# A merged attention-and-edge stage on one core: product buffers, a bank for projections, and the distance between steps

## The chip, the cores and the metric

The kernel runs on one core of one Trainium2 chip. A core has a matrix engine (PE, with its weight loads shown apart as PEld), a vector engine (DVE), a scalar engine (ACT), a general engine (POOL), and a sync engine (SP) that issues most of the direct DMAs here. The matrix engine writes its results to PSUM, which has eight banks of 2 KB in each of its 128 partitions. DVE and ACT read the results from there. The metric is the time of one execution on the device, in microseconds, as the median of several runs.

## The reference, cut to what matters

Two layers of a graph network work on 32768 nodes of 256 numbers and 524288 edges. The edges come sorted by `dst`.

```python
# layer 0: 256 graphs of 128 nodes, 8 heads of 32
h = relu(layernorm(x))
Q, K, V = h @ Wq + bq, h @ Wk + bk, h @ Wv + bv
attn = softmax(Q K^T / sqrt(32) + edge_bias)       # per graph and head; all edges fall to graph 0
x = x + (attn V) @ Wo + bo
# layer 1
h = relu(layernorm(x)); h = batchnorm(h)           # statistics over all nodes
a_in  = segment_sum((h @ W_in  + b_in )[src] * w_in,  dst)
a_out = segment_sum((h @ W_out + b_out)[dst] * w_out, src)
xi = concat(a_in, a_out) @ W_x2i + b_x2i;  hh = h @ W_h2h
gate = sigmoid(xi_i + hh_i); new = tanh(xi_n + hh_n)
x = x + new + gate * (h - new)
```

## The kernel before, in words

The kernel has four stretches. First it builds edge tables and the bias of graph 0. Then comes the merged stage, which the change is about. Then it adds up the messages per node, and at last it computes the gates.

The merged stage does two things at once. Attention works on groups of 512 nodes (`GB` = 4 graphs). The outgoing edges are handled at the same time: an *item* is 128 edges whose `dst` lie in one block of 128 nodes, 64 items (`CI`) make a round, and 4352 items are worked on in all. A loop of `turns` (L1133 onward) takes four rounds a trip (`UG`), or one. Each round carries the attention of one group (`attend`, L834) and the projections of the next group (`project`, L743), as long as groups are left; the last rounds have items alone. The edges come in three parts, and `spread` runs once for each.

Inside a trip the order of the work on PE, DVE, ACT and SP is written out by hand (`manual_schedule`); POOL is left out of that. The body is a Python loop over steps `t`, and one step starts one item. What an item needs is done at fixed lags, given by the tuple `steps` (L1130): at lag 0 SP fetches 128 rows of the normalised features (`fetch`, tile `hb`); at 4 PE spreads lane numbers to all partitions, for four items at once (`spread_lanes`, tile `bc`); at 6 DVE compares (`select`, tiles `selT` and `oh`); at 8 PE counts (`rank`), PE picks the rows of each edge (`product`, tile `mp`), and DVE reads the place of each edge (`place`, tile `jk`); at 9 ACT scales the product by the edge weight (`scale`, tile `msg`) and POOL scatters finished messages to memory (`scatter`). In one step, each engine runs what the tuple gives, from left to right, and then the attention work that `at(t)` put down for that step. An engine takes its instructions strictly in this order.

The places come from running counts `R`, which live in PSUM. There are two copies, in two tiles of their own, and item `i` uses copy `i % 2`. The rank of item `i` adds three matmuls to its copy:

```python
add("ones_b", i - 1, i, turn)     # R[i % 2] += all of item i - 1
add("triu", i - 2, i, turn)       # R[i % 2] += the rest of item i - 2
add("tri", i, i, turn)            # R[i % 2] += what stands before each edge of item i
```

Then `place` reads `R[i % 2]` on DVE. So the next matmul that touches the copy which item `i` reads is the first one of item `i + 2`.

PSUM is full: `mm`, `sc` and `pt` for attention and projections (one bank each), `bc`, two buffers of `mp`, and the two copies of `R`. The projections of the coming group borrow the banks of attention: transposed inputs and half of the queries and keys in `mm`, the other half in `pt`, values in `pt` and `sc`. In attention, a step's result is mostly read in the next step: scores (L849), their maximum (L857), the exponentials (L863), their transposes (L869), and so on.

Of the kernel before, what the change touches and what calls it, by code (L numbers as in the profile page):

```python
# [499 lines left out]
def gnn_kernel(ctx, tc, x, src, dst, edge_attr, edge_type, w_in_e, w_out_e,  # L500
# [186 lines left out]
    with ExitStack() as c1:  # L687
# [56 lines left out]
        def project(g, qT, kbd):  # L744
# [7 lines left out]
            for b in range(GB):  # L752
                cols = slice(b * P, (b + 1) * P)
                row = {}

                @at(9 + b // 2)
                def _(b=b):
                    row_stats(0, b, xg[:, b])

                @at(17 + 2 * b)  # L760
                def _(b=b, row=row):
                    xn = row["xn"] = ab.tile([P, D], F32, name="xn")
                    nc.vector.tensor_scalar(xn, xg[:, b], mv[0][:, b, 0:1], rstd[0][:, b:b + 1],
                                            op0=ALU.subtract, op1=ALU.mult)

                @at(18 + 2 * b)
                def _(row=row):
                    row["tp"] = transposed("mm", row["xn"])

                @at(19 + 2 * b)  # L770
                def _(row=row, cols=cols):
                    nc.scalar.activation(hT[:, :, cols], row["tp"], AF.Relu)
# [9 lines left out]
            for m in range(KC):  # L782
                ps = {}
                mc = slice(m * P, (m + 1) * P)
                bank = ("pt", "mm")[m]
                for k in range(KC):
                    @at(26 + 7 * m + k)
                    def _(m=m, k=k, ps=ps, mc=mc, bank=bank):
                        if k == 0:
                            ps["q"] = a_ps.tile([P, GN], F32, name=bank)  # L790
                        nc.tensor.matmul(ps["q"], wq[:, k, mc], hT[:, k], start=(k == 0), stop=(k == KC - 1))

                    @at(29 + 7 * m + k)
                    def _(m=m, k=k, ps=ps, mc=mc, bank=bank):
                        if k == 0:
                            ps["k"] = a_ps.tile([P, GN], F32, name=bank)
                        nc.tensor.matmul(ps["k"], wk[:, k, mc], hT[:, k], start=(k == 0), stop=(k == KC - 1))

                @at(28 + 7 * m)
                def _(m=m, ps=ps):  # L800
                    nc.scalar.activation(qT[:, m], ps["q"], AF.Identity, bias=bq_c[:, m:m + 1], scale=SCALE)

                for j in range(HC):
                    @at(31 + 7 * m + j // 2)
                    def _(m=m, j=j, ps=ps):
                        r = slice(j * DH, (j + 1) * DH)
                        to = kbd[r, m, :, j, :]
                        of = ps["k"][r].rearrange("p (b n) -> p b n", b=GB)
                        if j % 2:
                            nc.scalar.activation(to, of, AF.Identity, bias=bk_c[r, m:m + 1])  # L810
                        else:
                            nc.vector.tensor_scalar(to, of, bk_c[r, m:m + 1], None, op0=ALU.add)


            for b, t, bank in ((0, 41, "pt"), (2, 59, "sc")):
                ps = {}
                for i in range(2):
                    @at(t + i)
                    def _(b=b, i=i, ps=ps, bank=bank):
                        if i == 0:  # L820
                            ps["v"] = a_ps.tile([P, 2, D], F32, name=bank)
                        for k in range(KC):
                            nc.tensor.matmul(ps["v"][:, i], hT[:, k, (b + i) * P:(b + i + 1) * P], wv[:, k],
                                             start=(k == 0), stop=(k == KC - 1))

                @at(t + 2)
                def _(b=b, ps=ps):
                    nc.scalar.copy(vg[:, b:b + 2, :, 0:DH], ps["v"].rearrange("p b (h d) -> p b h d", d=DH))

            @at(63)  # L830
            def _():
                nc.gpsimd.tensor_add(xb, xg, bo_b[:, None, :].to_broadcast([P, GB, D]))
# [3 lines left out]
        def attend(g, qT, kbd, bias=None):  # L836

            todo, at = steps_of()
            for b in range(GB):
# [3 lines left out]
                for m in range(KC):  # L843
                    hs = slice(m * HC, (m + 1) * HC)

                    @at(B + 4 * m)
                    def _(b=b, m=m, s=s, cols=cols, hs=hs):
# [5 lines left out]

                    @at(B + 1 + 4 * m)
                    def _(m=m, s=s):
                        s["nm", m] = ab.tile([P, HC], F32, name="nm")
                        nc.vector.tensor_reduce(s["nm", m], s["sc", m], AX.X, ALU.max, negate=True)  # L857
                        s["pr", m] = ab.tile([P, HC, P], F32, name="pr")

                    for j in range(HC):  # L860
                        @at(B + (2, 6)[m] + j // 2)
                        def _(m=m, j=j, s=s):
                            nc.scalar.activation(s["pr", m][:, j], s["sc", m][:, j], AF.Exp, bias=s["nm", m][:, j:j + 1])  # L863

                        @at(B + (3, 7)[m] + j // 2)
                        def _(m=m, j=j, s=s):
# [3 lines left out]

                    @at(B + (6, 9)[m])
                    def _(m=m, s=s):
# [5 lines left out]

                    @at(B + 10 + m)
                    def _(b=b, m=m, s=s):  # L880
# [5 lines left out]

                @at(B + 12)
                def _(s=s):
# [19 lines left out]

                @at(B + 16)
                def _(b=b, s=s):  # L910
# [7 lines left out]

                @at(B + 17)
                def _(bs=bs):  # L920
                    std(1, bs)

                @at(B + 18)
                def _(bs=bs):
# [4 lines left out]
                for n, u in enumerate(range(bs.start, bs.stop)):  # L929
                    h = {}  # L930

                    @at(B + 18 + 2 * n)
                    def _(u=u):
                        nc.scalar.activation(h1g[:, u], x1g[:, u], AF.Relu, bias=nmr[:, u:u + 1], scale=rstd[1][:, u:u + 1])
# [9 lines left out]
            @at(B + 17)  # L944
            def _():
                nc.scalar.dma_start(x1_g[g], x1g)

            @at(B + 19)
            def _():
                nc.sync.dma_start(h1_g[g], h1g)  # L950

            @at(B + 21)
            def _():
# [35 lines left out]
        zm = fp.tile([P, T3 // P, MW], F32, name="zmsg")  # L989
        nc.vector.memset(zm, 0.0)  # L990
        nc.vector.memset(zm[:, :, FW:FW + 1], -1.0e6)
# [15 lines left out]
        def spread(k, lo, hi):  # L1007
# [7 lines left out]
            w0_1, node_1 = itp[k]  # L1015
            nc.scalar.dma_start(msg_d[k][hi - lo:hi - lo + T3].rearrange("(p e) w -> p e w", p=P), zm)
            for r in R:
                nc.tensor.matmul(r, cn["row0"], soff[k], start=True, stop=False, skip_group_check=True)

# [68 lines left out]
            def product(i, q, c, turn):  # L1088
                mp = turn["mp", i] = pp.tile([P, D], F32, name="mp")
                nc.tensor.matmul(mp, turn["sel", i // 4][:, q % 4], turn.pop(("hb", i)), start=True, stop=True)  # L1090

            def add(what, of, to, turn):
                oh = turn["oh", of]
                nc.tensor.matmul(R[to % 2], cn[what], oh, start=False, stop=False, skip_group_check=True)  # L1094

# [14 lines left out]
            def place(i, q, c, turn):  # L1110
                if q % 4 == 0:
                    c["pf"] = ip.tile([P, 4], F32, name="pf")
                jk = sp.tile([P, NB], F32, name="jk")
                nc.vector.scalar_tensor_tensor(jk, cn["iota1"], c["ed"][:, 0, q:q + 1], R[i % 2], op0=ALU.is_equal,  # L1114
                                               op1=ALU.mult, accum_out=c["pf"][:, q % 4:q % 4 + 1])
# [330 lines left out]
```

## Time and profile before

| what | us |
|---|---|
| median of 3 runs | 17105.49 (17104.96 to 17109.16) |
| the profiled execution | 19598.35 |
| its span, first to last instruction | 19596.6 |
| merged stage in the span, from and to | 1059 to 10047 |
| of it, rounds with attention (63) | 1059 to 9417 |
| of it, rounds of items alone (5) | 9417 to 10047 |
| a trip of four rounds with attention | 511 to 530 |
| a trip of one round, with attention / without | 128 to 149 / 122 to 126 |

The profiled execution takes 14.6% longer than the median run, so its times are not those of an ordinary run one by one. A row of the profile names the line of the kernel, the engine, what is written and read, how often, the busy time and the mean of one in nanoseconds, and then the time that the engine sat idle just before, with what ended most of that idle time. "issue" means that no wait visible to the profile ended there. PE's busy time counts the filling of its pipeline: matmuls that start 0.11 us apart are each shown with 0.27 us.

### The profile page before, as it was taken

To read this page: it belongs to the slowest core of one execution; us is meant where nothing else is said; L and a number is where in the kernel's file an instruction comes from. 1 tells how busy PE (TensorE), PEld (TensorE's weight loads), DVE (VectorE), ACT (ScalarE), POOL (GpSimd) and SP (SyncE) were. 2 spreads that over 40 slices of the span, in tenths; PEclk is the share of its full clock that TensorE was granted. 3 is DMA by queue.
4 is the path that set the end of the run, shared out by engine and by line. 5 is a ranking of instruction groups with operands and counts; after the bars stand their busy time and mean duration, and the time that the engine had idled before them with its cause. 6 is when DMAs were issued, how large, how long until landed. Compare 5 with 4: busy or idle time off the path is not lost. (4 is left out here: it accounts for less than half of the span.)

```text
span 19596.6 us, 292930 instructions
## 1 busy us (share of the span) xinstructions
PE 14917.0 (76%) x71786; PEld 10574.5 (54%) x71786; DVE 10035.6 (51%) x33823; ACT 6877.9 (35%) x17011; POOL 9326.3 (48%) x9309
## 2 busy tenths in 40 slices
PE   2078777777887777887668778777877777788889
PEld 2055555555555555555446666666666666653334
DVE  8656666566666656665444444444444444432222
ACT  0044444444444444444223333333333333320000
POOL 0045555445455445554555555555555555542222
PEclk6589989889888888988779999899999999999999
DMA  2044444444444434444446777677776777773332
GB/s 65 6 136 149 147 149 149 137 140 147 142 149 146 139 124 144 143 147 139 132 142 194 193 197 196 184 197 198 196 194 187 196 196 197 197 155 113 105 112 96
DMA packets 1829641, 2975.64 MB, mean 152 GB/s; under 512 B 299498, under 2 KB 1288135, under 8 KB 1827670
## 3 DMA queue, kind: packets, MB, share of 16 engines
q1 hardware_dynamic: 1203190, 1584.46, 27.5%
q0 software_dynamic: 430768, 1160.40, 20.5%
q10 hardware_dynamic: 194096, 212.95, 3.5%
q8 instruction: 590, 9.67, 0.2%
q14 instruction: 997, 8.17, 0.1%
HBM read 2124.16 MB, written 1248.64 MB: 172 GB/s over the span
## 5 line engine op out<-in xcount | busy, mean ns | idle before, releaser
L1123 POOL DMA_INDIRECT msg_d<-msg,pi x4352 | 4308.2, 990 | 3816.3 <-ACT msg L1106 1527.1
L1252 POOL DMA_INDIRECT rows<-h_d,ixc x3584 | 3407.5, 951 | 2331.8 <-issue 743.4
L1114 DVE SCALAR_TENSOR_TENSOR jk<-iota,edc,R 128x256 f32<-128x256 bf16 x4352 | 2072.8, 476 | 3059.3 <-remote 928.6
L1287 ACT ACTIVATE selo<-lane_row,sl 128x128 f32<-128x128 f32 x5040 | 1661.6, 391 | 4691.3 <-DVE sl L1284 1574.9
L1294 PE MATMUL ps_o<-m,selo 128*128 128x257 f32 x10080 | 2757.9, 413 | 645.7 <-ACT selo L1288 293.7
L1106 ACT ACTIVATE msg<-mp,edc 128x256 f32<-128x256 f32 x4352 | 2048.1, 477 | 3415.4 <-PE mp L1090 1522.5
L1266 PE MATMUL ps_i<-rows,sel 128*128 128x257 f32 x8960 | 2617.6, 412 | 761.6 <-DVE acc L1270 381.2
L1090 PE MATMUL mp<-hb,selT 128*128 128x256 f32 x8704 | 2926.6, 421 | 342.1 <-ACT msg L1106 145.7
L1294 PEld LDWEIGHTS ps_o<-m,selo 128*128 128x128 f32 x10080 | 1969.6, 205 | 1050.9 <-issue 312.5
L1266 PEld LDWEIGHTS ps_i<-rows,sel 128*128 128x128 f32 x8960 | 1627.5, 205 | 1054.7 <-DVE acc L1270 429.3
L1259 DVE TENSOR_SCALAR sel<-lane_row,ed 128x128 f32<-128x128 f32 x4480 | 1395.9, 360 | 973.2 <-PE idle L1267 374.7
L1090 PEld LDWEIGHTS mp<-hb,selT 128*128 128x128 f32 x8704 | 1460.2, 210 | 570.5 <-ACT msg L1106 230.9
L1094 PE MATMUL R<-oh,ones_b 128*128 128x256 bf16 x4352 | 1275.4, 293 | 635.6 <-issue 318.5
L1298 DVE SCALAR_TENSOR_TENSOR acc<-acc,blk,ps_o 128x257 f32<-128x257 f32 x1680 | 805.5, 479 | 1412.9 <-PE ps_o L1294 571.2
L1086 DVE TENSOR_SCALAR oh<-iota,edc 128x256 bf16<-128x256 bf16 x4352 | 1360.0, 313 | 2.0
L1094 PE MATMUL R<-oh,triu 128*128 128x256 bf16 x4352 | 1273.4, 293 | 10.5 <-DVE jk L1114 10.5
L1094 PE MATMUL R<-oh,tri 128*128 128x256 bf16 x4352 | 1272.2, 292 | 0.0
L1270 DVE SCALAR_TENSOR_TENSOR acc<-acc,blk,ps_i 128x257 f32<-128x257 f32 x2240 | 1070.0, 478 | 300.3 <-DMA sin_d<-acc 76.8
L1252 POOL DMA_INDIRECT rows<-h_d,ixh x896 | 852.2, 951 | 635.7 <-issue 247.2
L1284 DVE TENSOR_SCALAR sl<-m,blk 128x3 f32<-128x3 f32 x1680 | 416.6, 248 | 1372.4 <-DMA m<-msg_d 1139.5
L1094 PEld LDWEIGHTS <-triu 128*128 128x128 bf16 x4352 | 447.7, 103 | 1163.8 <-issue 1017.5
L1288 ACT ACTIVATE selo<-selo,one 128x384 f32<-128x384 f32 x1680 | 1031.1, 614 | 52.2
(372 smaller groups left out, 21051.9 us busy)
## 6 DMA issues: line engine op xcount, KB each, us to landing
m<-msg_d SPq DMA_DIRECT2D x1680, 396.0 KB
hb<-h_d SPq DMA_DIRECT2D x4352, 128.0 KB
sin_d<-acc SPq DMA_DIRECT2D x2240, 128.5 KB
sout_d<-acc SPq DMA_DIRECT2D x1680, 128.5 KB
msg_d<-msg,pi POOLq DMA_INDIRECT x4352
more<-sout_d ACTq DMA_DIRECT2D x128, 514.0 KB
rows<-h_d,ixc POOLq DMA_INDIRECT x3584
xg<-in_x SPq DMA_DIRECT2D x65, 512.0 KB
```

Of the source, the lines that this page charges most:

```text
L1086: nc.vector.tensor_scalar(oh, cn["iota1"], c["ed"][:, 0, q:q + 1], None, op0=ALU.is_equal)
L1090: nc.tensor.matmul(mp, turn["sel", i // 4][:, q % 4], turn.pop(("hb", i)), start=True, stop=True)
L1094: nc.tensor.matmul(R[to % 2], cn[what], oh, start=False, stop=False, skip_group_check=True)
L1106: nc.scalar.activation(msg[:, q % 4, 0:D], turn.pop(("mp", i)), AF.Copy, scale=c["ed"][:, 1, q:q + 1])
L1114: nc.vector.scalar_tensor_tensor(jk, cn["iota1"], c["ed"][:, 0, q:q + 1], R[i % 2], op0=ALU.is_equal, op1=ALU.mult, accum_out=c["pf"][:, q ...
L1123: s = nc.gpsimd.indirect_dma_start(out=msg_d[k][:], out_offset=bass.IndirectOffsetOnAxis(ap=c["pi"][:, j:j + 1], axis=0), in_=msgs[i // 4 ...
L1252: nc.gpsimd.indirect_dma_start(out=rows[(2 * i + r) % NR][:, 0:D], out_offset=None, in_=h1_d[:], in_offset=bass.IndirectOffsetOnAxis(ap=(i ...
L1259: nc.vector.tensor_scalar(sel[:, r], cn["lane_row"], c["ed"][:, 0, r, i:i + 1], c["ed"][:, 1, r, i:i + 1], op0=ALU.is_equal, op1=ALU.mult)
L1266: nc.tensor.matmul(ps, sel[:, r], rows[(2 * i + r) % NR], start=(r == 0), stop=(r == 1))
L1270: nc.vector.scalar_tensor_tensor(acc[0][i % NA], acc[0][(i - 1) % NA], c["blk"][:, 0, i:i + 1], c.pop(("t_ps", i)), op0=ALU.mult, op1=ALU.add)
L1287: nc.scalar.activation(sel[:, r], cn["lane_row"], AF.Abs, bias=sl[:, r:r + 1])
L1294: nc.tensor.matmul(ps, sel[:, r], m[:, r, 0:FW], start=(r == 0), stop=(r == T3 // P - 1))
```

## The change

The change touches the merged stage only.

- The product tile `mp` holds two products of 256 numbers, so that two tiles (two banks) hold four products. An even item takes a new tile, an odd one the second half of the same tile.
- The two copies of `R` become the halves of one tile, in one bank, written at the start by one matmul of 512 columns.
- The bank that this sets free is the tile `mx`. The projections (transposes, queries, keys, values) and the transposes of the normalised output rows use it and leave `mm`, `pt` and `sc` to attention.
- Rows are fetched 12 steps ahead of the product (`LEAD`), with 14 buffers in place of 10. The other lags keep their distance to the product.
- In `attend` and `project` two or three steps lie between an instruction that makes a value and the one on another engine that reads it, mostly in place of one.
- The one-hot tile `oh` has 7 buffers in place of 8, and the block of zeros `zm`, written once per part, is stored once and repeated by the DMA's pattern.

```diff
 # project
-                @at(17 + 2 * b)          # xn on DVE
+                @at(13 + 3 * b)
-                @at(18 + 2 * b)
+                @at(15 + 3 * b)
                 def _(row=row):
-                    row["tp"] = transposed("mm", row["xn"])
+                    row["tp"] = transposed("mx", row["xn"])
-                @at(19 + 2 * b)
+                @at(16 + 3 * b)
                 def _(row=row, cols=cols):
                     nc.scalar.activation(hT[:, :, cols], row["tp"], AF.Relu)
...
-                bank = ("pt", "mm")[m]
-                    @at(26 + 7 * m + k)
+                    @at(27 + 10 * m + k)
-                            ps["q"] = a_ps.tile([P, GN], F32, name=bank)
+                            ps["q"] = a_ps.tile([P, GN], F32, name="mx")
-                    @at(29 + 7 * m + k)
+                    @at(31 + 10 * m + k)
-                            ps["k"] = a_ps.tile([P, GN], F32, name=bank)
+                            ps["k"] = a_ps.tile([P, GN], F32, name="mx")
-                @at(28 + 7 * m)
+                @at(29 + 10 * m)
-                    @at(31 + 7 * m + j // 2)
+                    @at(33 + 10 * m + j // 2)
...
-            for b, t, bank in ((0, 41, "pt"), (2, 59, "sc")):
+            for b, t in ((0, 47), (2, 67)):
-            @at(63)
+            @at(67)
 # attend
-                    @at(B + 4 * m)                       # scores
+                    @at(B + 5 * m)
-                    @at(B + 1 + 4 * m)                   # maximum
+                    @at(B + 1 + 5 * m)
-                        @at(B + (2, 6)[m] + j // 2)      # exponentials
+                        @at(B + 2 + 5 * m + j // 2)
-                        @at(B + (3, 7)[m] + j // 2)      # transposes
+                        @at(B + 4 + 5 * m + j // 2)
-                    @at(B + (6, 9)[m])                   # copies PT
+                    @at(B + (6, 11)[m])
-                    @at(B + 10 + m)                      # attention times values
+                    @at(B + 12 + m)
-                @at(B + 12)                              # division
+                @at(B + 14)
-                @at(B + 13)                              # transposes
+                @at(B + 16)
-                @at(B + 14)                              # copy oT
+                @at(B + 17)
-                @at(B + 15)                              # times Wo
+                @at(B + 19)
-                @at(B + 16)                              # residual, statistics
+                @at(B + 20)
-                    @at(B + 18 + 2 * n)                  # normalised rows
+                    @at(B + 23 + 3 * n)
-                    @at(B + 19 + 2 * n)
+                    @at(B + 25 + 3 * n)
                     def _(u=u, h=h):
-                        h["tp"] = transposed("mm", h1g[:, u])
+                        h["tp"] = transposed("mx", h1g[:, u])
-                    @at(B + 20 + 2 * n)
+                    @at(B + 26 + 3 * n)
...
 # items
+        LEAD = 12
-        op = c1.enter_context(tc.tile_pool(name="p_o", bufs=8))
+        op = c1.enter_context(tc.tile_pool(name="p_o", bufs=7))
-        hp = c1.enter_context(tc.tile_pool(name="p_h", bufs=10))
+        hp = c1.enter_context(tc.tile_pool(name="p_h", bufs=14))
-        R = [p1.tile([P, NB], F32, name=f"R{i}") for i in range(2)]
+        R = p1.tile([P, 2, NB], F32, name="R")
...
-                mp = turn["mp", i] = pp.tile([P, D], F32, name="mp")
+                if i % 2 == 0:
+                    turn["mp"] = pp.tile([P, 2, D], F32, name="mp")
+                mp = turn["mp", i] = turn["mp"][:, i % 2]
...
-                nc.tensor.matmul(R[to % 2], cn[what], oh, start=False, stop=False, skip_group_check=True)
+                nc.tensor.matmul(R[:, to % 2], cn[what], oh, start=False, stop=False, skip_group_check=True)
...
-            steps = ((0, fetch), (4, spread_lanes), (6, select), (8, rank), (8, product), (8, place), (9, scale), (9, scatter))
+            steps = ((0, fetch), (LEAD - 4, spread_lanes), (LEAD - 2, select), (LEAD, rank), (LEAD, product), (LEAD, place),
+                     (LEAD + 1, scale), (LEAD + 1, scatter))
```

More of the change, by code (lines that the diff above doesn't have):

```diff
@@ L784, in project, with _ @@
                 mc = slice(m * P, (m + 1) * P)
-                bank = ("pt", "mm")[m]
                 for k in range(KC):
-                    @at(26 + 7 * m + k)
-                    def _(m=m, k=k, ps=ps, mc=mc, bank=bank):
+                    @at(27 + 10 * m + k)
+                    def _(m=m, k=k, ps=ps, mc=mc):
                         if k == 0:
-                            ps["q"] = a_ps.tile([P, GN], F32, name=bank)
+                            ps["q"] = a_ps.tile([P, GN], F32, name="mx")
                         nc.tensor.matmul(ps["q"], wq[:, k, mc], hT[:, k], start=(k == 0), stop=(k == KC - 1))
-                    @at(29 + 7 * m + k)
-                    def _(m=m, k=k, ps=ps, mc=mc, bank=bank):
+                    @at(31 + 10 * m + k)
+                    def _(m=m, k=k, ps=ps, mc=mc):
                         if k == 0:
-                            ps["k"] = a_ps.tile([P, GN], F32, name=bank)
+                            ps["k"] = a_ps.tile([P, GN], F32, name="mx")
                         nc.tensor.matmul(ps["k"], wk[:, k, mc], hT[:, k], start=(k == 0), stop=(k == KC - 1))
-                @at(28 + 7 * m)
+                @at(29 + 10 * m)
                 def _(m=m, ps=ps):
@@ L818, in _ @@
                     @at(t + i)
-                    def _(b=b, i=i, ps=ps, bank=bank):
+                    def _(b=b, i=i, ps=ps):
                         if i == 0:
-                            ps["v"] = a_ps.tile([P, 2, D], F32, name=bank)
+                            ps["v"] = a_ps.tile([P, 2, D], F32, name="mx")
                         for k in range(KC):
@@ L917, in attend @@
                 bs = slice(0, b + 1) if b < GB - 1 else slice(b, b + 1)
-                @at(B + 17)
+                @at(B + 21)
                 def _(bs=bs):
                     std(1, bs)
-                @at(B + 18)
+                @at(B + 22)
                 def _(bs=bs):
@@ L930, in attend @@
                     h = {}
-                    @at(B + 18 + 2 * n)
+                    @at(B + 23 + 3 * n)
                     def _(u=u):
                         nc.scalar.activation(h1g[:, u], x1g[:, u], AF.Relu, bias=nmr[:, u:u + 1], scale=rstd[1][:, u:u + 1])
-                    @at(B + 19 + 2 * n)
+                    @at(B + 25 + 3 * n)
                     def _(u=u, h=h):
-                        h["tp"] = transposed("mm", h1g[:, u])
-                    @at(B + 20 + 2 * n)
+                        h["tp"] = transposed("mx", h1g[:, u])
+                    @at(B + 26 + 3 * n)
                     def _(u=u, h=h):
                         nc.scalar.copy(h1T[:, :, u * P:(u + 1) * P], h["tp"])
-            @at(B + 17)
+            @at(B + 21)
             def _():
                 nc.scalar.dma_start(x1_g[g], x1g)
-            @at(B + 19)
+            @at(B + 24)
             def _():
                 nc.sync.dma_start(h1_g[g], h1g)
-            @at(B + 21)
+            @at(B + 28)
             def _():
@@ L988, in gnn_kernel @@
         p1 = c1.enter_context(tc.tile_pool(name="p_p1", bufs=1, space=PSUM))
-        zm = fp.tile([P, T3 // P, MW], F32, name="zmsg")
+        zm = fp.tile([P, MW], F32, name="zmsg")
         nc.vector.memset(zm, 0.0)
-        nc.vector.memset(zm[:, :, FW:FW + 1], -1.0e6)
+        nc.vector.memset(zm[:, FW:FW + 1], -1.0e6)
         eno = fp.tile([CI, T1], F32, name="eno")
         nc.gpsimd.iota(eno, pattern=[[1, T1]], base=0, channel_multiplier=0, allow_small_or_imprecise_dtypes=True)
-        R = [p1.tile([P, NB], F32, name=f"R{i}") for i in range(2)]
+        R = p1.tile([P, 2, NB], F32, name="R")
         win = fp.tile([CI, T1 * 4], F32, name="win")
@@ L1015, in spread @@
             w0_1, node_1 = itp[k]
-            nc.scalar.dma_start(msg_d[k][hi - lo:hi - lo + T3].rearrange("(p e) w -> p e w", p=P), zm)
-            for r in R:
-                nc.tensor.matmul(r, cn["row0"], soff[k], start=True, stop=False, skip_group_check=True)
+            nc.scalar.dma_start(msg_d[k][hi - lo:hi - lo + T3].rearrange("(p e) w -> p e w", p=P),
+                                zm[:, None, :].to_broadcast([P, T3 // P, MW]))
+            nc.tensor.matmul(R, cn["row0"], soff[k][:, None, :].to_broadcast([soff[k].shape[0], 2, NB]), start=True,
+                             stop=False, skip_group_check=True)
             def derive(c):
@@ L1113, in place @@
                 jk = sp.tile([P, NB], F32, name="jk")
-                nc.vector.scalar_tensor_tensor(jk, cn["iota1"], c["ed"][:, 0, q:q + 1], R[i % 2], op0=ALU.is_equal,
+                nc.vector.scalar_tensor_tensor(jk, cn["iota1"], c["ed"][:, 0, q:q + 1], R[:, i % 2], op0=ALU.is_equal,
                                                op1=ALU.mult, accum_out=c["pf"][:, q % 4:q % 4 + 1])
```

## The prediction, made before the changed kernel ran

> **What bounds the kernel now.** First I read the page's groups to see what a step costs, then the busy time by stretch, to place the merged stage.
>
> ```profile
> core 0: us, PE busy (x) PEld busy (x) DVE busy (x) ACT busy (x) POOL busy (x), PEclk, DMA share, GB/s
> 1058.00:3653.00 2595.00, 2075.19 (x11437) 1397.16 (x11437) 1621.60 (x5978) 1210.33 (x3021) 1325.69 (x1316) 0.91 0.47 149
> 10047.00:17400.00 7353.00, 5774.64 (x26865) 4863.27 (x26866) 3233.94 (x10368) 2648.05 (x6686) 4262.74 (x4485) 0.92 0.71 193
> ```
>
> The first row is five trips of four rounds: 2595 us for 20 rounds, so 129.7 us a round of 64 steps and 2.03 us a step. No engine is full: PE 80%, DVE 62%, POOL 51%, ACT 47%. The bound is in the waits. So next come the waits of PE between 1059 and 9418, where it stands idle 1754 us in all.
>
> ```profile
> PE R L1094 <- DVE jk L1114: 282.6, 205, 7.1
> PE R L1094 <- issue: 222.9, 118, 5.2
> PE sc L849 <- PEq L1135: 191.2, 15, 17.1
> PE pt L869 <- issue: 157.5, 91, 3.2
> PE mp L1090 <- ACT msg L1106: 137.5, 163, 2.3
> PE mm L741 <- DVE xn L763: 133.3, 40, 5.8
> PE mp L1090 <- issue: 96.3, 135, 2.4
> PE pt L869 <- ACT pr L863: 63.7, 90, 2.6
> PE mp L1090 <- ACT kbd L810: 63.0, 57, 1.8
> PE mm L741 <- ACT h1g L934: 62.7, 63, 3.5
> ...
> PE pt L869 <- ACT msg L1106: 37.4, 40, 2.0
> PE mm L741 <- DVE nm L857: 34.7, 28, 4.5
> ```
>
> Two kinds matter. PE waits for a result of the step before (xn, pr, h1g, nm; msg and kbd where ACT was late to free a product bank): the rows shown with a producer give 532 us, with o (18.3) and PT (10.8) 561 us. And its counting matmuls wait for DVE to have read R: 283 us, with only part of the 223 us of "issue". The rows of back-edges (191 us) the change leaves alone. Row fetches: in the whole stage PE idles 2.4 us for them, seven times.
>
> The last view is time order in rounds of items alone: the hand-over of R, both ways.
>
> ```profile
> 9707.09 0.27 PE L1094 MATMUL R<-oh,tri 128*128 128x256 bf16 x1
> 9707.40 0.48 DVE L1114 SCALAR_TENSOR_TENSOR jk<-iota,edc,R 128x256 f32<-128x256 bf16 x1
> ...
> 9712.14 0.48 DVE L1114 SCALAR_TENSOR_TENSOR jk<-iota,edc,R 128x256 f32<-128x256 bf16 x1 [3.75 <-remote]
> ...
> 9712.68 0.27 PE L1094 MATMUL R<-oh,ones_b 128*128 128x256 bf16 x1 [2.92 <-issue]
> ```
>
> From tri to DVE's read: 0.31 us. From the start of the read to the waiting matmul: 0.54. Three counting matmuls start 0.11 apart. A closed loop PE, DVE, PE thus takes 0.22 + 0.31 + 0.54 = 1.07 us. Today it may span two steps, because item i + 1 counts in another bank.
>
> **A rule of the skill, weighed.** The Trainium skill, "PSUM — Partial Sum Buffer", section "PSUM bank collisions raise a hardware error", says that two different engines must not be at one bank and one group of 32 partitions at once, even on disjoint columns, so software has to order them. The halves of the new R are disjoint columns of one bank on the same partitions. The trace of before shows the ordering done even more broadly: four reads of a key projection take different partitions of one bank, and ACT's reads follow DVE's, 0.03 to 0.09 us after they end. This is who waits for the DVE reads of L812:
>
> ```profile
> who waited for it (us, times):
>   ACT kbd L810: 430.7, 199
> ```
>
> I go by the rule: item i + 1 may not count before item i's place has been read. The three-matmul ping-pong stays, but the slack that it bought shrinks from two steps to one. The same holds for a product pair: ACT's scale of an even item must follow PE's product of the odd one.
>
> **The change, part by part**, against the profiled 19598 us (span 19597 and 2 around it), and then carried to the median.
>
> *R in one bank.* I lay the after schedule over 64 steps, with start-to-start pitches from the trace at full clock. PE: counting 3 x 0.109, product 2 x 0.216, spreading 0.22 every fourth step, scores 0.86, half of a block's attention 0.89, Wo 0.86, query or key part 0.86, a values part 0.86, a transpose 0.11. DVE: read 0.40, one-hot 0.19, selT 0.66 every fourth, maximum 0.59, PT 0.60, key copies 0.66 each, residual with statistics about 1.0, derive about 0.16 a step. PE sums to 86 us a round, DVE to 74. If neither can run ahead, a step costs the larger of PE, DVE and 1.07: the sum is 104.6. With today's schedule and pairs of steps, it is 97.2. The difference is 7.5 us a round, 0.12 us a step. A second reading agrees: among the 1555 steps whose read came within 0.6 us of tri, the next item's first matmul now starts before the point that the rule allows in 48%, by 0.12 us on the mean over all of them. Bounds: nothing, if product and attention (at least 0.43 us on PE) always cover the read; 104.6 - 86 = 18.6 us a round, 0.29 a step, if today's slack hides everything. I take 0.12 x 4352 = +507 us. Behind a waiting counting matmul stand the product, then the attention of that step; for the product waits ACT's scale, then POOL's scatter, which is idle half its time.
>
> *Steps farther apart, `mx`, four products.* These remove the 561 us at best (with the "issue" rows of pt, mp and mm, 315 us more, if they are the same thing); at worst nothing, as PE then meets the next wait. After the change PE has more work than DVE in 43 of 64 steps; in the others what it gains at a transpose it waits at the next counting. I take 0.6: -337 us. ACT waiting for the odd product costs nothing by itself: the attention results it makes later are read two steps on.
>
> *Twelve steps of lead.* The fetch is hidden already, so no gain. A trip has 4 more steps at its head with no counting; those carry attention, not waiting. At 26 trips and 0.4 us a light step: +42 us; from nothing to 100. SP issues the same 4352 fetches, four earlier, and the buffer of a fetch is freed two steps before in both versions (10 - 8, 14 - 12). POOL's scatters and window gathers are issued in the same order.
>
> *The rest.* Seven one-hot buffers leave three steps between last use and refill, covered by DVE's two steps of distance; the zeros are written three times in all; the wide first matmul of R happens three times. Nothing.
>
> Sum: 507 - 337 + 42 = +212 us on the profiled time. The median run is 14.6% shorter; the same share gives 212 / 1.146 = +185: 17,290 us. The forecast turns where R costs (337 - 42) / 4352 = 0.07 us a step.
>
> **Rivals.** A change within 0.2% (34 us) can't be told from none.
>
> 1. *Faster: the read is covered.* Attention on PE fills 0.6 us of a mean step beside the product's 0.43, and the read needs 0.84 us from tri, so most often DVE is done. R at 0.04 a step (174), all 561 gained, 42 added: -345, by 1.146 -301: 16,805. For it: the large number of producer waits. Against: DVE's own attention work stands ahead of the read in a third of the steps. It decides below 0.07 us a step.
> 2. *Faster: no ordering by bank.* If only the bytes touched count, R costs nothing: (-561 + 42) / 1.146 = -453: 16,650. The kbd rows speak against it.
> 3. *Much slower: lockstep.* R at its upper bound (1265 us) and gains of 0.4 (225): +1082, by 1.146 +944: 18,050. The Trainium skill's "TensorE: Matmul & The Clock Gate", section "HAM oscillation — how this bites in real kernels", adds a way to get there: PE gaps over about 3.4 us bring half clock. In the trace PE has 124 gaps over 3 us in this stretch and a clock of 0.91 to 0.84; in rounds of items alone it stands idle more and has 0.75. Waits of 0.5 us are too short for that by the page, so I give it little.
> 4. *Both cancel*: 17,105.
>
> **How the numbers follow.** Main case 0.44, rivals 0.28, 0.07, 0.12, 0.09 in that order. Faster 0.35, same 0.09, slower 0.56. The main case alone runs from 17,150 to 17,700. The range 16,760 to 18,000 leaves out most of rival 2 and half of rival 3.
>
> **What would show it.** In the profile after, PE's waits at L1094 for DVE jk grow from 283 us to over 700 with attention; the counting matmul follows the read of the item just before by 0.54 us in a third of the steps or more; PE's waits for xn, pr, h1g and for ACT msg at the product fall below half. A round takes 131 to 133 us. Rounds without attention get slower too, as they have the bank but nothing to gain. I am wrong if PE's waits for jk stay near 283 us, if a round falls under 128 us, or if the stretch after 10,047 us, whose code is the same, changes its length.

## The result, and the profile after

The changed kernel takes 17274.15 us (four runs, 17246.47 to 17293.5) against 17105.22 us (17091.69 to 17109.16). The ratio is 1.0099, with a 95% interval of 1.0085 to 1.0112: 169 us slower.

One thing has to be said before any two profiles are compared. The chips of this case fall into two kinds. On one kind the kernel before takes 17,105 to 17,364 us, on the other 19,598 to 19,672 us, timed or profiled alike. Each chip was used for one set of runs and kept its kind through it (on one of them, 31 runs of before lie between 19,648 and 19,701 us). Whether the kind belongs to the chip for good, or is a condition that outlasts one set, these runs cannot tell. The profile of before that the prediction was made from, with its 19,598 us, fits the slower kind in its time and in its waits, and the times beside it fit the quicker. So it was most likely no stretched picture of an ordinary run, as the text above had it, but a true one of another chip. Below, "quick" and "slow" name the kind, and every ratio of the tables compares two kernels on one chip. The profile after is of a quick chip. To have one of before to set beside it, before was run again on a quick chip.

PE's waits in the merged stage there, before. A row gives who waits for whom, then us in total, times, and the longest:

```profile
PE sc L849 <- PEq L1135: 221.2, 15, 19.8
PE pt L869 <- ACT pr L863: 174.3, 225, 1.9
PE mp L1090 <- ACT msg L1106: 167.5, 144, 1.8
PE mm L741 <- DVE xn L763: 117.8, 123, 1.5
PE R L1094 <- DVE jk L1114: 116.4, 101, 2.3
PE mm L741 <- ACT h1g L934: 83.2, 61, 3.2
```

And the same view after:

```profile
PE R L1097 <- DVE jk L1117: 633.4, 820, 1.8
PE sc L848 <- PEq L1139: 204.1, 15, 18.2
PE bc L1060 <- DVE selT L1085: 78.1, 63, 1.2
PE pt L868 <- ACT pr L862: 40.5, 42, 2.5
```

The waits for a result of the step before are almost gone: the exponentials `pr` fall from 174 to 41 us, and the rows for `msg` (168), `xn` (118) and `h1g` (83) are no longer among the leading ones. In their place stands one wait, for DVE to read R: 116 us before, 633 after. The groups of the page after say the same of the whole program: PE stands idle 2.5 us ahead of all products and 791 us ahead of the first counting matmuls.

```profile
L1093 PE MATMUL mp<-hb,selT 128*128 128x256 f32 x8704 | 2713.7, 395 | 2.5 <-DMA hb<-h_d 2.2
L1097 PE MATMUL R<-oh,ones_b 128*128 128x256 bf16 x4352 | 1215.9, 279 | 791.2 <-DVE jk L1117 662.5
```

The time order after shows how. The columns are start, duration, engine, line, and what is written from what:

```profile
2204.62 0.48 DVE L1117 SCALAR_TENSOR_TENSOR jk<-iota,edc,R 128x256 f32<-128x256 bf16 x1 [1.11 <-PE R L1097]
...
2205.16 0.27 PE L1097 MATMUL R<-oh,ones_b 128*128 128x256 bf16 x1
...
2205.80 0.47 DVE L1117 SCALAR_TENSOR_TENSOR jk<-iota,edc,R 128x256 f32<-128x256 bf16 x1
...
2206.34 0.27 PE L1097 MATMUL R<-oh,ones_b 128*128 128x256 bf16 x1 [0.25 <-DVE jk L1117]
```

Each first counting matmul starts 0.54 us after the read of the item just before (2204.62 to 2205.16, 2205.80 to 2206.34). Only the second is shown with a wait; ahead of the first, the product was still shown as running until 2205.02. The rows of waits thus undercount, and the time order of all 4352 items gives the fuller measure. In the changed kernel, the next item's first counting matmul starts 0.50 to 0.58 us after the read in 49% of the steps, and never sooner. In the kernel before, it does so in 0.2% of the steps, and in 54% it starts sooner than 0.50 us after the read or even ahead of it.

### The profile page after: what moved, and what is told of

It reads as the page before. It is cut to its first block, busy times and chain, and to the rows that moved or that the text cites. A ratio compares the mean times of both kernels' runs of the same rounds, so it can differ in the third digit from the quotient of the medians.

```text
span 17277.5 us, 290217 instructions
## 1 busy us (share of the span) xinstructions
PE 14126.0 (82%) x71780; PEld 10274.0 (59%) x71780; DVE 10214.7 (59%) x33823; ACT 6747.1 (39%) x17011; POOL 9318.6 (54%) x9309
## 5 line engine op out<-in xcount | busy, mean ns | idle before, releaser
L1109 ACT ACTIVATE msg<-mp,edc 128x256 f32<-128x256 f32 x4352 | 2006.3, 476 | 3495.3 <-PE mp L1093 3410.8
L1270 PE MATMUL ps_i<-rows,sel 128*128 128x257 f32 x8960 | 2499.1, 398 | 324.6 <-DVE acc L1274 248.9
L1298 PE MATMUL ps_o<-m,selo 128*128 128x257 f32 x10080 | 2568.3, 392 | 228.9 <-ACT selo L1292 225.3
L1093 PE MATMUL mp<-hb,selT 128*128 128x256 f32 x8704 | 2713.7, 395 | 2.5 <-DMA hb<-h_d 2.2
L1298 PEld LDWEIGHTS ps_o<-m,selo 128*128 128x128 f32 x10080 | 1867.7, 195 | 541.6 <-ACT selo L1292 184.1
L1270 PEld LDWEIGHTS ps_i<-rows,sel 128*128 128x128 f32 x8960 | 1563.5, 198 | 575.3 <-DVE acc L1274 355.9
L1097 PE MATMUL R<-oh,ones_b 128*128 128x256 bf16 x4352 | 1215.9, 279 | 791.2 <-DVE jk L1117 662.5
L1093 PEld LDWEIGHTS mp<-hb,selT 128*128 128x128 f32 x8704 | 1369.7, 198 | 67.5 <-DMA hb<-h_d 4.4
L1097 PE MATMUL R<-oh,tri 128*128 128x256 bf16 x4352 | 1217.8, 280 | 0.0
L1097 PE MATMUL R<-oh,triu 128*128 128x256 bf16 x4352 | 1204.4, 278 | 0.0
```

Of the source, the lines that this page charges most:

```text
L1097: nc.tensor.matmul(R[:, to % 2], cn[what], oh, start=False, stop=False, skip_group_check=True)
L1109: nc.scalar.activation(msg[:, q % 4, 0:D], turn.pop(("mp", i)), AF.Copy, scale=c["ed"][:, 1, q:q + 1])
L1270: nc.tensor.matmul(ps, sel[:, r], rows[(2 * i + r) % NR], start=(r == 0), stop=(r == 1))
L1298: nc.tensor.matmul(ps, sel[:, r], m[:, r, 0:FW], start=(r == 0), stop=(r == T3 // P - 1))
```

## The experiments

### First set: what is R worth, and what is the rest worth?

Four kernels went to one chip, and the changed kernel to a second; both were chips of the second kind.

Before, unchanged.

> The kernel before, unchanged, for a second profile. The profile after has a span of 17277 us, that of its ordinary runs, while the first profile of before was 14.6% longer than its runs and its last two stretches, whose code does not change, were longer too. If the stretching was an event of that one execution: a span near 17105 us, a stretch after the merged stage of some 6100 us as after the change (7350 in the first profile), and the waits of PE for xn, pr, h1g, nm and for ACT msg still there with 350 to 560 us. If it belongs to the kernel: a span near 19600 us again.

It took 19647.22 us, so the longer time was no event of one execution. The waits for jk (296 us), xn (132) and msg (143) are those of the first profile (283, 133, 138).

Before, with only the two copies of R put into one bank:

```diff
-        R = [p1.tile([P, NB], F32, name=f"R{i}") for i in range(2)]
+        R = p1.tile([P, 2, NB], F32, name="R")
-                nc.tensor.matmul(R[to % 2], cn[what], oh, ...
+                nc.tensor.matmul(R[:, to % 2], cn[what], oh, ...
-                nc.vector.scalar_tensor_tensor(jk, cn["iota1"], c["ed"][:, 0, q:q + 1], R[i % 2], ...
+                nc.vector.scalar_tensor_tensor(jk, cn["iota1"], c["ed"][:, 0, q:q + 1], R[:, i % 2], ...
```

> The kernel before, with the two copies of R made halves of one tile in one bank, and nothing else. Theory (item i + 1 may not count before item i's place is read): 0.10 to 0.12 us a step, 440 to 510 us, so 17,540 us (17,350 to 17,700), with PE's waits at the counting matmuls for DVE's read at 650 us or more. Rival (product and attention cover the read, and the loss of the change comes from elsewhere): within 50 us of 17,105, and waits near those of before.

Ratio 1.0025 (1.0016 to 1.0034): hardly slower here, a tenth of what was expected, although the hand-over is now held in 51% of the steps (0.6% in before) and the jk waits are 796 us.

After, with R in two banks again. The bank for that comes from `mx`: the projections go back into attention's banks, at places where these are free.

```diff
-                    row["tp"] = transposed("mx", row["xn"])
+                    row["tp"] = transposed("pt" if b < 2 else "mm", row["xn"])
-                            ps["q"] = a_ps.tile([P, GN], F32, name="mx")
+                            ps["q"] = a_ps.tile([P, GN], F32, name=("sc", "mm")[m])
-                            ps["k"] = a_ps.tile([P, GN], F32, name="mx")
+                            ps["k"] = a_ps.tile([P, GN], F32, name=("pt", "sc")[m])
-            for b, t in ((0, 47), (2, 67)):
+            for b, t, bank in ((0, 47, "pt"), (2, 67, "mm")):
-                        h["tp"] = transposed("mx", h1g[:, u])
+                        h["tp"] = transposed("mm" if b == GB - 1 else "sc", h1g[:, u])
-        R = p1.tile([P, 2, NB], F32, name="R")
+        R = [p1.tile([P, NB], F32, name=f"R{i}") for i in range(2)]
```

> The changed kernel with the two copies of R in banks of their own again; the projections and the transposes of normalised rows go to the attention's three banks, each where that bank is free in the new order of steps, since no eighth bank is left. Theory: what R in one bank costs comes back, 17,274 - 440 = 16,830 us (16,650 to 17,000), faster than both kernels. Rival (the loss comes from the longer lead or from the steps' new places): 17,200 to 17,350. If the bank for projections were what pays: above 17,350.

Ratio 1.0015 (1.0008 to 1.0022). All of the change but R gains nothing on this chip, where a gain was expected. PE's waits at the counting matmul, in the same window as below:

```profile
PE R L1097 <- DVE jk L1117: 635.9, 377, 6.6
PE R L1097 <- issue: 325.4, 219, 5.2
```

Here R has two banks, and only 0.6% of the steps are held as described above. Yet PE waits 636 us for jk, against 296 in before. So on this kind of chip the farther places alone move waits to the counting matmul, and a large jk row does not by itself show that the bank is the cause.

After, with a single R. Each item adds two matmuls in place of three, and counting follows the read item by item anyway:

```diff
-        R = p1.tile([P, 2, NB], F32, name="R")
+        R = p1.tile([P, NB], F32, name="R")
-                    add("ones_b", i - 1, i, turn)
-                if i > 1:
-                    add("triu", i - 2, i, turn)
+                    add("triu", i - 1, i, turn)
```

> The changed kernel with one copy of R and two counting matmuls an item in place of three (the rest of item i - 1, then what stands before each edge of item i). The order PE, DVE, PE is the same as with two halves of one bank, but PE has 0.109 us less to do a step, and the closed loop is shorter by as much. Theory (lockstep, PE the longer engine in two thirds of the steps): 0.07 us a step, -318 us, 16,960 us (16,800 to 17,100). Rival (PE alone sets the pace, DVE's read is covered): the whole 0.109 us, -474 us, 16,800 us. If DVE and the hand-over set the pace: within 50 us of 17,274.

Ratio 1.0114 (1.0097 to 1.0131). Set against the whole change on the other slow chip (1.0201, next), that is some 0.9% less, about half of what was expected.

The changed kernel itself, on the other slow chip:

> The changed kernel, unchanged, beside the kernel before on one chip. The chip of the first four runs takes 19,672 us for the kernel before, and PE pauses there 3 to 5 us about every 104 matmuls and weight loads, which the profile after (17,277 us) does not show. If this chip is of the quick kind: a ratio of 1.010 as before. If it is of the slow kind, theory: the pauses cover part of the hand-over, as PE is the one that is late, so the ratio lies nearer to 1 (0.995 to 1.006: R in one bank alone gave 1.0025 there); rival: pauses and lockstep add up, 1.015 or more.

It took 20053.39 against 19642.3 us: 1.0201 (1.0184 to 1.0218), so twice the loss of the quick chip. I had held that the two nearly free parts would stay nearly free together; that fell. PE's waits there (window 1059 to 9400), for R in one bank alone and then for the whole change:

```profile
PE R L1094 <- DVE jk L1114: 796.3, 587, 5.9
PE R L1094 <- issue: 216.2, 176, 4.9
```

```profile
PE R L1097 <- DVE jk L1117: 983.5, 852, 7.0
PE R L1097 <- issue: 444.6, 334, 5.6
```

The waits at the counting matmul (both rows together) are 511 us in before, 961 with the new places and R apart, 1012 with R in one bank in the old places, and 1428 with both. Either part alone only put these waits in the place of others: PE's idle time in the stage was 1997 us in before, 1943 and 1973. With both, it was 2291. The single R of the run before this one costs less with the same new places (1.0114), though the two ratios are of two chips: as long as the read holds the next item, the third matmul and the second half of R are only more work for PE.

### Second set: the small parts alone, on a quick chip

All four are made from before, so the old places of the steps stay.

Four products in the same two banks:

```diff
-                mp = turn["mp", i] = pp.tile([P, D], F32, name="mp")
+                if i % 2 == 0:
+                    turn["mp"] = pp.tile([P, 2, D], F32, name="mp")
+                mp = turn["mp", i] = turn["mp"][:, i % 2]
```

> The kernel before with the product tiles of two halves (four products in the same two banks), and nothing else. On a chip of the slow kind PE waits 143 us for ACT msg and 67 us for ACT kbd at the product. Theory (waits of PE shift to the next one more than they vanish): 0 to -100 us, ratio 0.995 to 1.000. Rival (they are won in full): -200 us, ratio 0.990. A third case: the scale of an even item now follows the product of the odd one, which makes ACT late and costs more: above 1.001.

It took 17457.37 against 17348.79 us: 1.0064 (1.0047 to 1.0081), slower, as in the third case of the expectation. PE's waits with it:

```profile
PE pt L869 <- ACT pr L863: 330.0, 258, 2.3
...
PE mm L741 <- ACT h1g L934: 126.3, 126, 3.7
```

The wait of the product for `msg` is gone (168 us), but those for ACT's results grow by 199 us (330 against 174 for `pr`, 126 against 83 for `h1g`). What ACT itself waits for, first with pairs and then in before, with us and times:

```profile
  PE mp L1092: 2704.3, 1660
```

```profile
  PE mp L1090: 2005.0, 2168
```

ACT reads an even product only when PE has written the odd one into the same bank: it never starts sooner than 0.42 us after the start of the odd product's last matmul, while in before it is ahead of that matmul in 86% of the pairs. It waits 699 us more at the product, and its attention work comes after that.

Twelve steps of lead, with the buffers that belong to it:

```diff
-        hp = c1.enter_context(tc.tile_pool(name="p_h", bufs=10))
+        hp = c1.enter_context(tc.tile_pool(name="p_h", bufs=14))
-            steps = ((0, fetch), (4, spread_lanes), (6, select), (8, rank), (8, product), (8, place), (9, scale), (9, scatter))
+            steps = ((0, fetch), (8, spread_lanes), (10, select), (12, rank), (12, product), (12, place), (13, scale), (13, scatter))
```

Seven one-hot buffers and the single block of zeros are in it too.

> The kernel before with rows fetched 12 steps ahead, 14 row buffers, 7 one-hot buffers and the single block of zeros, and nothing else. Theory (fetches hidden already, four more light steps at the head of 26 trips): +20 to +100 us, ratio 1.001 to 1.005. Rival on a chip of the slow kind (the pauses of PE are late rows after all): the pauses get fewer, -200 us or more, ratio below 0.990. Rival in the other direction (the lead is the main loss of the change): +200 us or more.

It took 17513.81 us: 1.0097 (1.0080 to 1.0113), the rival's price and not the forecast one. The stage has 26 trips. Between the last item's count in a trip and the first item's in the next (both taken at the matmul with `tri`), 632 us pass in before, over all 25 borders, and 762 with the lead: 5.2 us more at each. Inside the trips, from the first count to the last, the sum is 7153 us in before and 7173 with the lead. (The profile of before is from the next set, of a chip within 3 us of this one's.) So most of the loss comes once a trip, where the next trip has to start up. The one-hot buffers turn over at every item, and can hardly have cost more than the 20 us inside the trips.

Before with a single R (the edit shown above), two counting matmuls an item:

> The kernel before with one copy of R and two counting matmuls an item: the order PE, DVE, PE of the changed kernel, with the old places of the steps, and 0.109 us less on PE a step. Theory: R in one bank cost 50 us here on the slow kind, and the third matmul was worth 160 us between the changed kernel and the one with one R, so -110 us, ratio 0.992 to 0.997; on a quick chip about 0, 0.990 to 1.010. Rival (lockstep costs what the matmul saves): 1.000 or more.

It took 17442.28 us: 1.0056 (1.0039 to 1.0073), inside the wide range for a quick chip, with 643 us of waits for jk.

The same, and product pairs in three banks, using the bank that became free:

> The same with product tiles of two halves in three banks (the bank that one R sets free), six products. Theory: as the four products alone show, added to the kernel with one R: ratio 0.987 to 0.997. Rival: once item i + 1 waits for item i's read, PE can't run ahead of ACT by more than a step, so more products can't help: within 0.002 of the kernel with one R.

It took 17572.85 us: 1.0124 (1.0107 to 1.0141). Both expectations missed: even six products lose, 0.7% on top of the single R, as much as four products lost alone. This points to the pair in one bank, not to the number of buffers.

### Third set: R alone and the rest alone, on a quick chip

Before, as the profile to compare with:

> The kernel before, unchanged, for its profile on the chip of this call. On a quick chip: a merged stage of 7800 to 7850 us (what is left of 17,349 us when the first 1060 us and the 8465 us behind the stage, equal in three kernels on that chip, are taken off), and no pauses of PE at every eighth item. PE's waits for pr, xn, h1g and for ACT at the product sum to 400 to 700 us, those for DVE's read to 100 to 250 us. On a chip of the slow kind: the profile known already.

It took 17363.95 us, and its waits are shown with the result.

Before, with R in one bank:

> The kernel before with the two copies of R in one bank, on the chip of this call. On a quick chip, theory: what one R and two matmuls cost there (+0.56%), and on top the part of the third matmul that PE pays for (0.04 to 0.11 us an item, 160 to 470 us): ratio 1.015 to 1.033. Rival (the new bank costs 50 us as on the slow kind, and the loss of the change is the lead's, +0.97% alone): 1.001 to 1.005. On the slow kind 1.0025 again.

It took 17679.64 against 17351.86 us: 1.0185 (1.0168 to 1.0202), or 328 us between the medians, as the theory had it. PE's waits:

```profile
PE R L1094 <- DVE jk L1114: 639.4, 545, 3.7
...
PE mm L741 <- DVE xn L763: 61.9, 62, 1.3
PE pt L869 <- ACT pr L863: 43.2, 90, 1.6
```

No step of the attention was moved here, and yet the wait for `pr` falls from 174 to 43 us and that for `xn` from 118 to 62. PE waits at the counting instead, and what it waited for later is ready by then. So a falling row is no proof that farther places did it.

The busy time of the merged stage, in before and with R in one bank (length, then PE's busy time):

```profile
1063.00:8849.00 7786.00, 6472.23 (x37980) 4467.21 (x37979) 5464.59 (x20079) 3959.22 (x9929) 4499.86 (x4463) 0.94 0.51 164
```

```profile
1060.00:9156.00 8096.00, 6700.95 (x37964) 4554.94 (x37964) 5544.77 (x20071) 3977.28 (x9928) 4507.09 (x4472) 0.93 0.49 158
```

The stage is 310 us longer for the same instructions, and 229 us of that is shown as PE being busy. The clock (0.94 to 0.93) can be worth some 70 us of it, an estimate from 6472 us of busy time. The rest fits the drain of a matmul that nothing follows at once: it is shown with 0.27 us where its successor may start after 0.11. This is inferred from the way these matmuls are shown.

After, with R in two banks:

> The changed kernel with R in two banks and the projections in the attention's banks, on the chip of this call. On a quick chip, theory (R in one bank is the main loss): 0.985 to 1.000. Rival (lead and product pairs, +0.97% and +0.64% alone, are the loss, and the new places of the steps gain what R costs): 1.008 or more. On the slow kind 1.0015 again.

It took 17057.37 against 17351.86 us: **0.9832 (0.9815 to 0.9848), 294 us faster** than before, a little more than expected, and the only kernel of this study that is faster than before. PE's waits:

```profile
PE R L1097 <- DVE jk L1117: 201.9, 227, 2.5
...
PE pt L868 <- ACT kbd L809: 93.8, 63, 1.5
...
PE pt L868 <- ACT pr L862: 59.7, 145, 1.9
```

The `kbd` row (94 us) comes from having no bank for projections: the transposes wait until ACT has read a key projection out of `pt`. PE's idle time in the stage is 1026 us (before 1314, after 1320), and the stage takes 7464 us (7785 and 7921).

All runs together. The stage goes from the first counting matmul to the last read; "held" is the share of steps whose counting starts 0.50 to 0.58 us after the read of the item before:

| kernel | chip | us | ratio to before (95%) | stage, us | PE idle in it | held |
|---|---|---|---|---|---|---|
| before | quick | 17363.95 | – | 7785 | 1314 | 0.2% |
| R in one bank | quick | 17679.64 | 1.0185 (1.0168–1.0202) | 8096 | 1395 | 48% |
| one R, two matmuls | quick | 17442.28 | 1.0056 (1.0039–1.0073) | 7854 | 1574 | 49% |
| one R, six products | quick | 17572.85 | 1.0124 (1.0107–1.0141) | 8007 | 1660 | 46% |
| four products | quick | 17457.37 | 1.0064 (1.0047–1.0081) | 7895 | 1384 | 0.3% |
| lead of 12 | quick | 17513.81 | 1.0097 (1.0080–1.0113) | 7937 | 1382 | 0.2% |
| the whole change | quick | 17274.15 | 1.0099 (1.0085–1.0112) | 7921 | 1320 | 49% |
| the change, R in two banks | quick | 17057.37 | 0.9832 (0.9815–0.9848) | 7464 | 1026 | 1.4% |
| before | slow | 19647.22 | – | 8969 | 1997 | 0.6% |
| R in one bank | slow | 19722.29 | 1.0025 (1.0016–1.0034) | 9024 | 1973 | 51% |
| the change, R in two banks | slow | 19700.19 | 1.0015 (1.0008–1.0022) | 9014 | 1943 | 0.6% |
| the change, one R | slow | 19891.23 | 1.0114 (1.0097–1.0131) | 9195 | 2413 | 51% |
| the whole change | slow | 20053.39 | 1.0201 (1.0184–1.0218) | 9375 | 2291 | 56% |

The chip of the whole change's quick row ran before in 17105 us; the chips of the other quick rows in 17349 and 17352 us. Between rows of different chips, the ratios are what can be compared. Most of the gap between the quick chips lies behind the merged stage, in code that the change leaves alone: 8276 us on the chip of the whole change, 8513 in before on the other. Taken off 17,105 us with the 1063 us ahead of the stage, it leaves an estimated 7766 us for the stage of before there, within 20 us of the row above. So the quick rows can be compared by their stage times too.

## Why the prediction was right, step by step

The forecast of 17,290 us and the time of 17274 us lie 16 us apart, and the main case came in: the wait for R took more than the other parts gave. How far each step held is another matter.

**R in one bank: right, mechanism and size.** The loop came as described: the hand-over in 0.54 us, in about half of the steps (a third or more was forecast), and the counting of the next item never ahead of the read. This agrees with the rule of the Trainium skill's "PSUM — Partial Sum Buffer", section "PSUM bank collisions raise a hardware error", that the forecast went by: disjoint halves of a bank were ordered all the same. That also settles rival 2, in which only the bytes count; it would have shown steps below 0.50 us, and there are none. The order is kept by semaphores of the program, on which PE waits until DVE is done. What the runs do not separate is the bank from the tile as its reason: every PSUM tile of the stage has a bank of its own, so two halves of one bank were always two halves of one tile as well. The forecast was +507 us in the profiled execution, 442 when carried to the median. On quick chips the whole change stands at 1.0099 and the change with R apart at 0.9832; the ratio of the two is 1.027, some 463 us on 17,352. The stage times say the same: 7921 against 7464 us. This compares two chips and holds `mx` as well: with R apart there is no bank for it. In the old places, R alone costs 328 us on one chip. In us per item that is 0.11 and 0.075, against 0.12 / 1.146 = 0.10 forecast and a turn at 0.07 / 1.146 = 0.06. (The forecast's 507 us are 0.1165 us a step; with the rounded 0.12 they would be 522.)

**The rest: right as a sum, wrong in its parts.** Spacing, `mx`, products and lead were to give (-337 + 42) / 1.146 = -257 us. Measured, without `mx`: -294. But two terms were mis-sized:

- *Twelve steps of lead: +42 us (37 carried over), "from nothing to 100".* Alone it measured +165 us (0.97%). The step was "26 trips and 0.4 us a light step", and the 0.4 had no measurement behind it; a border between trips shows 5.2 us for four steps more, not 1.6.
- *Four products: "ACT waiting for the odd product costs nothing by itself".* Alone they measured +109 us (0.64%). The reason given, that ACT's later results are read two steps on, does not hold in the old places, where these results are read one step on. Whether it holds in the new ones was not run apart.

As the rest gained 294 us all the same, the new places must gain more than the 0.6 of 561 us that the prediction took, if the two parts cost there what they cost alone. But parts do not simply add here: on the slow chips +0.25% and +0.15% made +2.0%. New places alone, with R apart, a lead of 8 and single products, were not run, so this division stays open.

**The base and the scaling: wrong.** The sum of +212 us was made against 19,598 us and then divided by 1.146, as if that execution were an ordinary one made longer. On the kind of chip that it fits, the change costs 2.01% or some +395 us, almost twice the sum. There the rest costs 29 us, where it was to gain 295, and R on top of it (1.0201 / 1.0015, two chips) 366, where 507 stood in the sum; in the old places, R in one bank costs 50. What the sum described was the quick chip, whose waits for results (some 600 us in the rows of before) happen to be close to the 561 us read from the other kind. That the total met the quick chip within 16 us is therefore in part luck: the lead and the products, each alone, lost more than was put in, the rest of the change made up for it, and the division by 1.146 had no ground.

**Signs in the profile.** Waits for jk "from 283 us to over 700": 984 on a slow chip, 633 on a quick one, where before had 116. On the slow chip this sign says little, as the change with R in two banks has 636 there; on a quick one it has 202. Waits for xn, pr, h1g and msg below half: seen, but R in one bank alone does most of that for xn and pr. "A round takes 131 to 133 us": in trips of four, 134 to 138 on a slow chip, where before has 129 to 132, and 114 to 118 on a quick one, where before has 113 to 116. By the letter, two signs of being wrong came: a round is under 128 us, and the stretch behind the stage takes 8276 us, where the first profile has 9558. Both belong to the kind of chip and not to the change. On one quick chip that stretch takes 8513, 8520 and 8512 us in three kernels, so it did not change.

"Rounds without attention get slower too": not on a quick chip, and here the prediction missed what sets the pace. From a round's first count to its last, some 59 us pass in before and some 75 with R in one bank, alone or with the whole change; so the counting did get slower. But a round as a whole stays at 95 to 98 us in before and with R in one bank alone, and at 98 to 99 with the whole change. POOL's scatters fill it. First in before, then after:

```profile
8578.73 0.98 POOL L1123 DMA_INDIRECT msg_d<-msg,pi  x1 [0.30 <-issue]
8580.02 0.98 POOL L1123 DMA_INDIRECT msg_d<-msg,pi  x1 [0.30 <-issue]
```

```profile
8686.27 0.98 POOL L1126 DMA_INDIRECT msg_d<-msg,pi  x1 [0.30 <-issue]
8687.56 0.98 POOL L1126 DMA_INDIRECT msg_d<-msg,pi  x1 [0.31 <-issue]
```

They start 1.29 us apart, and 64 of them take 83 us, to which the change of trips is added. The prediction read POOL as "idle half its time" from its busy share; that share leaves out the 0.30 us between two scatters.

**The rivals.** The first (the read is covered) fell with the 49% of held steps. The third (lockstep at its bound) would have given 18,050 us: half of the steps are held, not all. The fourth (both cancel) is outside the interval of the ratio, 1.0085 to 1.0112.

## What to carry to other kernels

An accumulator that one engine adds to while another reads it wants a tile in a bank of its own for each copy: here two copies in one bank were one copy for the order of the work, and then the extra matmul that keeps two of them bought nothing (on two quick chips, one copy with two matmuls lost 0.56%, two halves with three lost 1.85%). A bank is better taken from a use that can wait, here the projections, than from a hand-over that closes every step. Before a sum is made from a profile, its time is to be set beside the times of the runs; where they differ by far more than the runs do among themselves, as by 14.6% here, it may be of a chip with other limits, and terms cannot be scaled from one to the other. And a busy share is no measure of how much room an engine has left, when its instructions never start closer than their length and a gap.

## What the runs showed of the hardware

- **Two kinds of chip.** The same program takes 17,105 to 17,364 us on some chips and 19,598 to 19,672 us on others. The difference is not confined to one stage: behind the merged stage, before takes 9615 us on a slow chip and 8513 on a quick one. On the slow chips, in rounds of items alone, PE often stands still for 3 to 5 us; in the first profile, 13 of 28 gaps over 2.6 us came exactly eight items after the one before, and the prediction's time order has one of them (before the counting matmul at 9712.68, with DVE idle 3.75 us). On the quick chips PE stands still that long only between two rounds. The granted clock of PE in these rounds is 0.75 in before and 0.77 after on slow chips, 0.83 and 0.89 on quick ones. What causes the pauses is open.
- **Scatters on POOL.** A scatter is shown busy for 0.98 us, and the next one starts 1.29 us after it, also where it waits for nothing that the profile shows.
- **A part's price depends on its chip.** R in one bank costs 1.85% on a quick chip and 0.25% on a slow one, while the whole change costs 0.99% and 2.01%. On the slow chip the wait for R alone mostly replaces other waits (PE idle 1973 us against 1997), and so do the new places alone (1943); that explains the small numbers, but why the two parts together cost eight times as much as R alone there was not settled.
